# A planned two-layer graph kernel on one core: other landing costs and no chain between transfers in the plan, another form of one gated update, and one gate moved ahead

## The chip, the core and the metric

The kernel runs on one core of a Trainium2 chip. The metric is device microseconds of one launch, as the median of a few runs; lower is better. A core has five engines that work side by side, each through its own list of instructions in order: PE (TensorE, matrix products), DVE (VectorE), ACT (ScalarE), POOL (GpSimd) and SP (SyncE, which here only issues transfers). Transfers (DMAs) are issued by SP, ACT or POOL and then run by themselves; an engine that needs the data waits for a semaphore. Because each list is worked in order, an instruction that waits also holds up everything behind it on the same engine.

## What is computed

Thirty-two sequences `x[b]` of 512 nodes with 128 features go through two layers that share one 512 x 512 adjacency matrix. Layer 0 is a graph attention layer, layer 1 a gated graph network of five steps. Each has a layer norm and a ReLU in front and a residual sum behind. Cut to what matters:

```python
h = jnp.maximum(_layernorm(x, axis=-1), 0.0)
x = x + _L0_gnn_ref(h, adj, ...)              # softmax over neighbours, then a weighted mean
h = jnp.maximum(_layernorm(x, axis=-1), 0.0)
def step(h, _):                               # five times
    m_in = jnp.einsum('nm,bmd->bnd', in_matrix, h)
    m_out = jnp.einsum('nm,bmd->bnd', out_matrix, h)
    av = jnp.concatenate([m_in, m_out], axis=-1)
    u3 = h @ u3_w.T + u3_b
    z = jax.nn.sigmoid(av @ w3_w.T + w3_b + u3)
    r = jax.nn.sigmoid(av @ w4_w.T + w4_b + u3)
    hv = jnp.tanh(av @ w5_w.T + w5_b + (r * h @ u5_w.T + u5_b))
    h = (1.0 - z) * h + z * hv
    return (h, None)
x = x + h
```

Both matrices of the second layer are the same adjacency matrix, so the kernel forms one product `m` and adds the weight halves beforehand.

## The kernel before

**One step of one sequence.** A step is called by `recurrence(b, step, ...)` (L1012); below, (8, 1) means sequence 8, step 1. The state is kept twice: as `hT` (features in the partitions, f32, scaled by `LIFT`), and as rows split into two f16 parts, `hi` and `lo`, whose sum stands for the f32 value. In order, a step does this:

- PE: `m` from four products with `hi` and four with `lo` (L1031). ACT copies it to `mT` (L1042).
- PE: the r gate, `g` from `u3T` with `hT` and `w4sT` with `mT` (L1050, L1051). ACT takes its tanh, `rs` (L1056). DVE makes `rh` (L1063).
- PE: the z gate, by adding `w3dT` with `mT` onto the same bank once `rs` has been read (L1071). ACT takes its tanh, `zs` (L1078).
- PE: the candidate `v` from `w5sT` with `mT` and `u5hT` with `rh` (L1089, L1090). ACT takes its tanh, `hv` (L1095).
- DVE: three full-width instructions, `d = LIFT*hv - hT` (L1101), `d = (zs+1)*d` (L1107), `hT = 0.5*d + hT` (L1110). The gates are tanh forms, so that (tanh+1)/2 is the sigmoid.
- The new `hT` must be turned back into rows for the next step's `hi` and `lo` (L1008, L1006).

The turning is done in two ways. In the first steps and in the last two steps of the last four sequences, PE transposes `hT` into a PSUM bank (L1124). Everywhere else (146 times) it goes by way of DRAM: DVE transposes blocks of 32 (L1137, `blocks`), SP stores them to a DRAM buffer (L1143, `way`), and SP loads them back in four parts (L1148, `rows`). After the last step the result is scaled by `1/LIFT`, added to the kept input `x1s` and stored (L1172 to L1188).

**Layer 0** of a sequence (`layer0`, L763) feeds the recurrence. From the fifth sequence on its transposes also go through DRAM, issued by POOL: `blockwise` (L717) stores four parts (L733) and loads them back (L746), and the attention scores are spread with four small stores (L866) and one load (L879).

**The last sequence** ends in `ending` (L1191) in halves. Its result is summed in a PSUM bank: `kept`, the part `(zs-1)*hT` (L1201), is turned by products with the matrix `minus` (L1211); `gated`, the part `(zs+1)*hv` (L1234), is turned by products with `plus` (L1241).

**What sets the order.** No order is written out by hand. `add` collects tasks, each with an engine, a cost from `COST`, a key, its needs and its buffers. `plan` (L83) then plays them through and puts out the order in which they begin. At each turn it looks, engine by engine, for tasks whose needs are met and whose buffers are free, and takes among those that can begin soonest the one with the lowest key. A task's result counts as seen at its planned end plus `lands`; for a transfer that is `LANDING`, 2600 ns (L48):

```python
seen = begin + t.ns + t.lands
...
heir.at = max(heir.at, begin + t.ns if heir.engine == t.engine == "PE" else seen)
```

The order so found is then pinned on every engine. It is only an order: on the chip each instruction waits for its true needs, not for the planned time. In the plan each of the four loads of `rows` needs the load before it to have landed:

```python
needs.append(add("SP", [1], keys(6), load(g), (t, *needs[-1:]), (way, f),
                 lands=LANDING))
```

and the four stores of `blockwise` (L742) and of the scores (L875) are chained in the same way. On the chip no such wait exists, since the parts don't touch each other; the chain only spreads them out in the order.

Of the kernel before, what the change touches and what calls it, by code (L numbers as in the profile page):

```python
# [13 lines left out]
ALU = mybir.AluOpType  # L14

P = 128
# [6 lines left out]
LIFT = 4096.0  # L23
# [4 lines left out]
SLOTS = 10  # L28
# [6 lines left out]
EARLY_NORMS = ("a1", "a2", "a3", "b0")  # L35
ADJ_LANDS = 5600
HALVED = 1
STEP = 6100
LEAD = 11
COST = {  # L40
# [4 lines left out]
    "SP": (430, 0, 0),  # L45
}
FIRST_IDLE, IDLE = 32, 36
LANDING = 2600  # L48
BRANCH = 150

WAIT = {"DVE": 200, "ACT": 200}
# [232 lines left out]
def gat_then_gated_gnn_kernel(  # L284
# [20 lines left out]
    nc = tc.nc  # L305
    B, N, D = x.shape
    K = N // P
# [14 lines left out]
    pin = tc.keep_in_program_order  # L322
    tasks = []

    def add(*args, **kwargs):
        tasks.append(Task(*args, **kwargs))
        return tasks[-1]

    def new(buffer, name, shape=(P, N)):
        tag = buffer.tags[0]  # L330
        if "bank" in buffer.tags:
            buffer.tile = psum.tile([P, N], F32, tag="bank", name=name)
        elif tag in ("way", "turn", "line"):
# [35 lines left out]
    x1s = [state.tile([P, K, D], F32, name=f"x1_{s}") for s in range(SLOTS)]  # L369
# [85 lines left out]
    t = add("PE", [1024], soon, issue, (a_dst_loaded,), (f_as,), at=4300)  # L455
# [56 lines left out]
    t = add("POOL", [1] * 3, 0, issue, (rest_loaded,))  # L512
# [9 lines left out]
    t = add("PE", [256] * 5, 0, issue, (t,), (f_ws, f_us))  # L522
# [55 lines left out]
    t = add("DVE", [1] * 4, late, issue, (*counted, wa_made))  # L578
# [138 lines left out]
    def blockwise(dst, src, which, keys, needs, buffers, by_halves):  # L717


        f, way = Buffer("blocks"), Buffer("turn")  # L720

        def blocks():
            pin(nc.vector.transpose(
                new(f, f"blocks_{which}"), src().rearrange("p k d -> p (k d)")
            ))

        t = add("DVE", [512], keys(0), blocks, needs, (*buffers, f))

        def store(g):
            def issue():  # L730
                if way.tile is None:
                    new(way, f"turn_{which}", (K * P, P))
                pin(nc.gpsimd.dma_start(  # L733
                    out=way.tile.rearrange("(e r) (g q) -> g r e q", r=Q, g=G)[g],
                    in_=f.tile[ts(g, Q)].rearrange("r (e q) -> r e q", q=Q),
                ))

            return issue

        stores = []  # L740
        for g in range(G):
            stores.append(add("POOL", [1], keys(1), store(g), (t, *stores[-1:]), (f, way),  # L742
                              lands=LANDING))

        def load():
            pin(nc.gpsimd.dma_start(  # L746
                out=dst().rearrange("p (k m) -> p k m", k=K),
                in_=way.tile.rearrange("(k p) m -> p k m", k=K),
            ))

        return add("POOL", [1], keys(2), load, stores, (*buffers, way), lands=LANDING + 1500)

    finished = {}

    def due(b):

# [6 lines left out]
    def layer0(b):  # L763
# [7 lines left out]
        def keys(i):  # L771
            return begin + length * (base[0] + i) / parts
# [61 lines left out]
        if direct:  # L834
            f_es = Buffer("g", "bank")

            def spread(half):
                def issue():
                    es = f_es.tile or new(f_es, f"es_{b}")
                    for k in range(2 * half, 2 * half + 2):  # L840
                        pin(nc.tensor.transpose(
                            es[:, ts(k, P)], hw()[:, k, D + 1 : D + 2].to_broadcast([P, P]), ident
                        ))

                return issue

            t = None
            for half in range(2):
                t = add("PE", [256] * 2, keys(0), spread(half), (made[half], t), (f_hw, f_es))
        else:  # L850
            f_es, f_lines, way = Buffer("es"), Buffer("lines"), Buffer("line")
            rep = Q // K

            def gather():
                pin(nc.vector.transpose(
                    new(f_lines, f"lines_{b}", (P, Q)).rearrange("p (k e) -> p k e", k=K),
                    hw()[:, :, D + 1 : D + 2].to_broadcast([P, K, rep]),
                ))

            t = add("DVE", [64], keys(0), gather, made, (f_hw, f_lines))  # L860

            def store(k):
                def issue():
                    if way.tile is None:
                        new(way, f"line_{b}", (K, P))
                    pin(nc.gpsimd.dma_start(  # L866
                        out=way.tile[k].rearrange("(g q) -> g q", g=G),
                        in_=f_lines.tile[k * rep :: Q],
                    ))

                return issue

            stores = []
            for k in range(K):
                stores.append(add("POOL", [1], keys(1), store(k), (t, *stores[-1:]),  # L875
                                  (f_lines, way), lands=LANDING))

            def spread():
                pin(nc.gpsimd.dma_start(  # L879
                    out=new(f_es, f"es_{b}"),  # L880
                    in_=way.tile.rearrange("k p -> (k p)").partition_broadcast(P),
                ))

            t = add("POOL", [1], keys(2), spread, stores, (way, f_es), lands=LANDING + 1500)
        base[0] = 15
# [126 lines left out]
    def recurrence(b, step, halved, turned):  # L1012
# [5 lines left out]
        def keys(i):  # L1018
            return key + i * STEP / 4

        hT = hTs[b % SLOTS]
# [51 lines left out]
            ))  # L1073

        t = add("PE", [2048], keys(3), gate_z, (t_r,), (f_g, f_mT))

        def tanh_z():
            pin(nc.scalar.activation(  # L1078
# [11 lines left out]
            pin(nc.tensor.matmul(v, lhsT=u5hT, rhs=f_rh.tile, start=False, stop=True))  # L1090

        t = add("PE", [2048] * 2, keys(3), candidate, (t_rh,), (f_v, f_mT, f_rh))

        def tanh_v():
            pin(nc.scalar.activation(new(f_hv, f"hv_{b}_{step}"), f_v.tile, AF.Tanh, bias=vb))  # L1095

        t = add("ACT", [512], keys(4), tanh_v, (t,), (f_v, f_hv))


        def differ():  # L1100
# [8 lines left out]
        def update():  # L1109
            pin(nc.vector.scalar_tensor_tensor(hT, f_d.tile, 0.5, hT, ALU.mult, ALU.add))  # L1110

        t = add("DVE", [512], keys(5), differ, (t,), (f_hv, f_d))
        t = add("DVE", [512], keys(5), gated, (t, t_z), (f_z, f_d))
        turned = add("DVE", [512], keys(5), update, (t,), (f_d,))

        nth = 5 * b + WIDTH * step
        if nth < 5 * SHORT or (step >= STEPS - 2 and b >= B - SHORT_END):

            f = Buffer("o", "bank")

            def turn():
                h_ps = new(f, f"h_{b}_{step}")
                for k in range(K):
                    pin(nc.tensor.transpose(h_ps[:, ts(k, P)], hT[:, ts(k, P)], ident))  # L1124

            needs = (add("PE", [256] * K, keys(6), turn, (turned,), (f,)),)
            view = ("p k d -> p k d", {})

            def src():
                return f.tile.rearrange("p (k d) -> p k d", k=K)  # L1130
        else:


            f_b, way, f = Buffer("blocks"), Buffer("way"), Buffer("rows")

            def blocks():
                pin(nc.vector.transpose(  # L1137
                    new(f_b, f"blocks_{b}_{step}").rearrange("p (g k q) -> p g k q", g=G, k=K),
                    hT.rearrange("p (k g q) -> p g k q", g=G, k=K),
                ))  # L1140

            def store():
                pin(nc.sync.dma_start(out=new(way, f"way_{b}_{step}"), in_=f_b.tile))  # L1143

            def load(g):
                def issue():
                    rows = f.tile or new(f, f"rows_{b}_{step}", (P, G, N // G))
                    pin(nc.sync.dma_start(  # L1148
                        out=rows[ts(g, Q)],
                        in_=way.tile.rearrange("(a q) (g e) -> g q a e", a=G, g=G)[g],  # L1150
                    ))

                return issue

            t = add("DVE", [512], keys(6), blocks, (turned,), (f_b,))
            t = add("SP", [1], keys(6), store, (t,), (f_b, way), lands=LANDING)
            needs = []
            for g in range(G):
                needs.append(add("SP", [1], keys(6), load(g), (t, *needs[-1:]), (way, f),
                                 lands=LANDING))  # L1160
            view = ("p k (a q) -> p a k q", {"a": G})

            def src():
                return f.tile.rearrange("p a (k q) -> p a k q", k=K)
# [11 lines left out]

        def result_at_once():
            pin(nc.vector.scalar_tensor_tensor(
                new(f_res, f"res_{b}", (P, K, D)), src(), 1 / LIFT, x1s[b % SLOTS], ALU.mult,
                ALU.add,  # L1180
            ))

        if view[1]:
# [148 lines left out]
```

## Time and profile before

| what | value |
|---|---|
| median of three runs | 1145.57 us (1143.91 to 1149.21) |
| the profiled execution, its own time | 1144.8 us |
| its span, first to last instruction | 1142.7 us |
| PE busy | 1133.5 us (99%), 4373 instructions |
| DVE busy | 940.6 us (82%), 2124 instructions |
| ACT busy | 659.9 us (58%), 1297 instructions |
| POOL busy | 350.0 us (31%), 503 instructions |
| granted TensorE clock, mean | 1.000 |
| SP's transfers, by packets' time | 26.5% of 16 DMA engines |
| POOL's transfers, by packets' time | 13.0% of 16 DMA engines |
| `way` stores, `rows` loads | 146 of 256 KB, 584 of 64 KB |

Busy time is counted from the records of one execution on the chip. A wait names what came last before the engine went on. Matmul records overlap, since they are pipelined; a long stretch of busy PE says that nothing kept it waiting, not that it ran at its peak.

### The profile page before, as it was taken

The numbers are of one execution on the slowest core, as the hardware profiler recorded it, in microseconds if no ns is written. First come the engines' busy times: TensorE is split into PE (matmuls) and PEld (weight loads), VectorE is DVE, ScalarE is ACT, GpSimd is POOL, SyncE is SP. The second block draws the span as 40 slices with busy tenths as digits, with TensorE's granted clock in tenths as the row PEclk, the third lists the DMA queues.
The fourth block names the chain that finished last, engine by engine and source line by source line (L and its number), as shares of the span: only waits on it lengthen the run. The fifth ranks groups of instructions, "written<-read, shape, count | busy, mean of one in ns | idle before, by whom it ended". The sixth has DMA issues, their size and how long they took to land.

```text
span 1142.7 us, 15158 instructions
## 1 busy us (share of the span) xinstructions
PE 1133.5 (99%) x4373; PEld 598.5 (52%) x4373; DVE 940.6 (82%) x2124; ACT 659.9 (58%) x1297; POOL 350.0 (31%) x503
## 2 busy tenths in 40 slices
PE   9999999999999999999999999999999999999998
PEld 8665554554555545555554555555555555444444
DVE  7888887887879979889898888799889988667664
ACT  6665656456556465647556646655655655555553
POOL 4345434123244143244413242432544331100000
PEclk9999999999999999999999999999999999999999
DMA  3114444344354444344543443452455343322311
GB/s 107 44 38 122 115 128 133 112 146 118 104 164 116 136 130 136 116 138 119 146 136 115 126 132 120 139 154 89 133 149 144 116 121 117 107 92 79 102 44 67
DMA packets 133916, 132.88 MB, mean 116 GB/s; under 512 B 22083, under 2 KB 97989, under 8 KB 133701
## 3 DMA queue, kind: packets, MB, share of 16 engines
q1 hardware_dynamic: 116066, 94.89, 26.5%
q0 software_dynamic: 17472, 36.79, 13.0%
q8 instruction: 36, 0.59, 0.2%
q14 instruction: 52, 0.42, 0.1%
q10 hardware_dynamic: 290, 0.20, 0.1%
HBM read 70.39 MB, written 61.40 MB: 115 GB/s over the span
## 4 chain that ended last, share of the span: by engine, by line
PE 91%; DVE 5%; DMA 2%; issue 1%; ACT 0%; SPq 0%; DVEq 0%; ACTq 0%
PE m L1031 23%; PE g L1071 11%; PE v L1090 11%; PE g L1050 11%; PE v L1089 11%; PE g L1051 11%; PE av L922 9%; PE hp L806 2%; DMA rows<-way 1%; DVE hT L1110 1%; DVE pt L891 1%; DVE blocks L1137 1%; DVE lo L1006 1%; PE h L1124 1%; DVE d L1101 0%
## 5 line engine op out<-in xcount | busy, mean ns | idle before, releaser
L1056 ACT ACTIVATE rs<-g,zrb 128x512 f32<-128x512 f32 x160 | 109.7, 686 | 143.9 <-PE g L1051 133.4
L1101 DVE SCALAR_TENSOR_TENSOR d<-hv,hT 128x512 f32<-128x512 f32 x159 | 108.4, 682 | 78.3 <-ACT hv L1095 78.0
L1095 ACT ACTIVATE hv<-v,vb 128x512 f32<-128x512 f32 x159 | 108.8, 684 | 104.8 <-PE v L1090 104.2
L1042 ACT COPY mT<-m 128x512 f32<-128x512 f32 x160 | 93.6, 585 | 123.7 <-PE m L1031 121.1
L1031 PE MATMUL m<-adjT,hi 128*128 128x512 f16 x640 | 162.6, 379 | 1.8 <-ACT hi L1008 1.8
L1050 PE MATMUL g<-hT,u3T 128*128 128x512 f32 x320 | 163.5, 593 | 0.0
L1051 PE MATMUL g<-mT,w4sT 128*128 128x512 f32 x320 | 163.5, 592 | 0.0
L1071 PE MATMUL g<-mT,w3dT 128*128 128x512 f32 x320 | 163.1, 593 | 0.0
L1031 PE MATMUL m<-adjT,lo 128*128 128x512 f16 x640 | 162.1, 379 | 0.4 <-DVE lo L1006 0.4
L1089 PE MATMUL v<-mT,w5sT 128*128 128x512 f32 x318 | 162.4, 592 | 0.0
L1090 PE MATMUL v<-rh,u5hT 128*128 128x512 f32 x318 | 162.4, 592 | 0.0
L1078 ACT ACTIVATE zs<-g,zrb 128x512 f32<-128x512 f32 x160 | 109.6, 686 | 59.6 <-PE g L1071 56.6
L1063 DVE SCALAR_TENSOR_TENSOR rh<-rs,hT 128x512 f32<-128x512 f32 x160 | 108.6, 682 | 40.8 <-ACT rs L1056 40.3
L922 PEld LDWEIGHTS av<-hw,pt 128*128 128x128 f32 x1024 | 122.0, 191 | 17.8 <-issue 13.6
L922 PE MATMUL av<-hw,pt 128*128 128x129 f32 x1024 | 123.2, 275 | 0.2 <-ACT adjT L497 0.2
L1110 DVE SCALAR_TENSOR_TENSOR hT<-d,hT 128x512 f32<-128x512 f32 x159 | 109.7, 690 | 11.3
L1031 PEld LDWEIGHTS <-hi 128*128 128x128 f16 x640 | 62.5, 98 | 103.0 <-issue 46.7
L1107 DVE SCALAR_TENSOR_TENSOR d<-zs,d 128x512 f32<-128x512 f32 x159 | 109.6, 689 | 4.5
L1137 DVE STREAM_TRANSPOSE blocks<-hT 128x512 f32<-128x512 f32 x146 | 102.7, 706 | 5.3 <-DMA way<-blocks 3.2
L1031 PEld LDWEIGHTS <-lo 128*128 128x128 f16 x640 | 62.4, 98 | 84.7 <-issue 14.2
L644 POOL TENSOR_TENSOR rs_b<-ve_b,mhalf 128x4 f32<-128x4 f32 x32 | 37.2, 1162 | 224.7 <-DVE ve_b L624 188.4
L1051 PEld LDWEIGHTS g<-mT,w4sT 128*128 128x128 f32 x320 | 60.7, 190 | 76.7 <-issue 71.5
(135 smaller groups left out, 1443.7 us busy)
## 6 DMA issues: line engine op xcount, KB each, us to landing
way<-blocks SPq DMA_DIRECT2D x146, 256.0 KB, 2.1
rows<-way SPq DMA_DIRECT2D x584, 64.0 KB, 2.1
x<-in_x_dram SPq DMA_DIRECT2D x32, 256.0 KB, 2.9
out_dram<-res SPq DMA_DIRECT2D x31, 256.0 KB, 2.1
turn_a<-blocks_a POOLq DMA_DIRECT2D x112, 64.0 KB, 2.3
h0T<-turn_a POOLq DMA_DIRECT2D x28, 256.0 KB, 3.5
es<-line POOLq DMA_DIRECT2D x28, 256.0 KB, 3.8
turn_b<-blocks_b POOLq DMA_DIRECT2D x112, 64.0 KB, 2.3
```

What stands on the lines that cost most here:

```text
L922: pin(nc.tensor.matmul(avs()[:, i, :], lhsT=f_pts[c].tile[:, ts(2 * part + i, P)], rhs=hw()[:, c, : D + 1], start=start, stop=(c == K - 1) ...
L1031: pin(nc.tensor.matmul(f_m.tile, lhsT=part[:, k, :], rhs=adjT[:, k, :], start=(first and k == 0), stop=(not first and k == K - 1),))
L1050: pin(nc.tensor.matmul(g, lhsT=u3T, rhs=hT, start=True, stop=False))
L1051: pin(nc.tensor.matmul(g, lhsT=w4sT, rhs=f_mT.tile, start=False, stop=True))
L1056: pin(nc.scalar.activation(new(f_r, f"rs_{b}_{step}"), f_g.tile, AF.Tanh, bias=rb, scale=0.5))
L1071: pin(nc.tensor.matmul(f_g.tile, lhsT=w3dT, rhs=f_mT.tile, start=False, stop=True, skip_group_check=True))
L1078: pin(nc.scalar.activation(new(f_z, f"zs_{b}_{step}"), f_g.tile, AF.Tanh, bias=zb, scale=0.5))
L1089: pin(nc.tensor.matmul(v, lhsT=w5sT, rhs=f_mT.tile, start=True, stop=False))
L1090: pin(nc.tensor.matmul(v, lhsT=u5hT, rhs=f_rh.tile, start=False, stop=True))
L1107: pin(nc.vector.scalar_tensor_tensor(d, f_z.tile, 1.0, d, ALU.add, ALU.mult))
L1110: pin(nc.vector.scalar_tensor_tensor(hT, f_d.tile, 0.5, hT, ALU.mult, ALU.add))
L1137: pin(nc.vector.transpose(new(f_b, f"blocks_{b}_{step}").rearrange("p (g k q) -> p g k q", g=G, k=K), hT.rearrange("p (k g q) -> p g k q", ...
```

## The change

Three things are changed.

- **The plan's transfers.** `LANDING` goes from 2600 to 5000 ns, for all transfers that use it. The chain is taken off the four loads of `rows`, off the four stores of `blockwise` and off the four score stores: each now needs only the data it moves. All orders of all engines come out of the plan anew.
- **The update of sequence 30 in its last step** (`near`; sequence 31 takes `ending`). Instead of `d`, `d`, `hT`, three instructions in a row of which the first needs `hv`, it makes `kept = (zs-1)*hT` as soon as `zs` is there, then `hv = (zs+1)*hv`, then `kept = LIFT*hv - kept`. That is twice the new state; it is turned from the `d` buffer, and the result is scaled by `0.5/LIFT`.
- **The last sequence's z gate** in the last step becomes a need of sequence 30's candidate, so that PE does it first.

```diff
+NEAR = 2
...
-LANDING = 2600
+LANDING = 5000
...
-            stores.append(add("POOL", [1], keys(1), store(g), (t, *stores[-1:]), (f, way),
+            stores.append(add("POOL", [1], keys(1), store(g), (t,), (f, way),
                               lands=LANDING))
...
-                stores.append(add("POOL", [1], keys(1), store(k), (t, *stores[-1:]),
+                stores.append(add("POOL", [1], keys(1), store(k), (t,),
                                   (f_lines, way), lands=LANDING))
...
         t = add("PE", [2048], keys(3), gate_z, (t_r,), (f_g, f_mT))
+        if last and b == B - 1:
+
+            candidates[b - 1].needs.append(t)
+            candidates[b - 1].missing += 1
+            t.heirs.append(candidates[b - 1])
...
         t = add("PE", [2048] * 2, keys(3), candidate, (t_rh,), (f_v, f_mT, f_rh))
+        candidates[b] = t
...
+        near = last and b >= B - NEAR
...
-        t = add("DVE", [512], keys(5), differ, (t,), (f_hv, f_d))
-        t = add("DVE", [512], keys(5), gated, (t, t_z), (f_z, f_d))
-        turned = add("DVE", [512], keys(5), update, (t,), (f_d,))
+
+
+        def keep():
+            pin(nc.vector.scalar_tensor_tensor(
+                new(f_d, f"kept_{b}"), f_z.tile, -1.0, hT, ALU.add, ALU.mult
+            ))
+
+        def gated_hv():
+            hv = f_hv.tile
+            pin(nc.vector.scalar_tensor_tensor(hv, f_z.tile, 1.0, hv, ALU.add, ALU.mult))
+
+        def twice():
+            pin(nc.vector.scalar_tensor_tensor(
+                f_d.tile, f_hv.tile, LIFT, f_d.tile, ALU.mult, ALU.subtract
+            ))
+
+        if near:
+            t_keep = add("DVE", [512], keys(3.5) - STEP, keep, (t_z,), (f_z, f_d))
+            t = add("DVE", [512], keys(5), gated_hv, (t, t_z), (f_z, f_hv))
+            turned = add("DVE", [512], keys(5), twice, (t, t_keep), (f_hv, f_d))
+            to_turn = f_d
+        else:
+            t = add("DVE", [512], keys(5), differ, (t,), (f_hv, f_d))
+            t = add("DVE", [512], keys(5), gated, (t, t_z), (f_z, f_d))
+            turned = add("DVE", [512], keys(5), update, (t,), (f_d,))
+            to_turn = None
...
-                needs.append(add("SP", [1], keys(6), load(g), (t, *needs[-1:]), (way, f),
+                needs.append(add("SP", [1], keys(6), load(g), (t,), (way, f),
                                  lands=LANDING))
...
-                new(f_res, f"res_{b}", (P, K, D)), src(), 1 / LIFT, x1s[b % SLOTS], ALU.mult,
-                ALU.add,
+                new(f_res, f"res_{b}", (P, K, D)), src(), (0.5 if near else 1) / LIFT,
+                x1s[b % SLOTS], ALU.mult, ALU.add,
```

More of the change, by code (lines that the diff above doesn't have):

```diff
@@ L751, in blockwise @@
         return add("POOL", [1], keys(2), load, stores, (*buffers, way), lands=LANDING + 1500)
-    finished = {}
+    finished, candidates = {}, {}
     def due(b):
@@ L1122, in turn @@
                 h_ps = new(f, f"h_{b}_{step}")
+                h = to_turn.tile if to_turn else hT
                 for k in range(K):
-                    pin(nc.tensor.transpose(h_ps[:, ts(k, P)], hT[:, ts(k, P)], ident))
-            needs = (add("PE", [256] * K, keys(6), turn, (turned,), (f,)),)
+                    pin(nc.tensor.transpose(h_ps[:, ts(k, P)], h[:, ts(k, P)], ident))
+            needs = (add("PE", [256] * K, keys(6), turn, (turned,),
+                         (f, to_turn) if to_turn else (f,)),)
             view = ("p k d -> p k d", {})
```

## The prediction

> **What bounds the kernel now.** I read the page first (shares, granted clock, chain), then PE's waits, then the timeline round the longest wait on three engines, then the end.
>
> ```profile
> PE 1133.5 (99%) x4373; PEld 598.5 (52%) x4373; DVE 940.6 (82%) x2124; ACT 659.9 (58%) x1297; POOL 350.0 (31%) x503
> ...
> PE 91%; DVE 5%; DMA 2%; issue 1%; ACT 0%; SPq 0%; DVEq 0%; ACTq 0%
> ```
>
> ```profile
> PE m L1031 <- ACT hi L1008: 1.8, 1, 1.8
> PE idle L434 <- POOL ident masks.py:199: 1.4, 1, 1.4
> PE m L1031 <- DVE lo L1006: 0.4, 1, 0.4
> PE h L1124 <- DVE hT L1110: 0.2, 1, 0.2
> PE av L922 <- ACT adjT L497: 0.2, 1, 0.2
> ```
>
> PE is the bound, at a clock of 1.000, and is idle for 4.0 us in five places (columns: total, times, longest). What remains of the 9.2 us between PE's busy time and the span is the 5.2 us after its last product: the last results on DVE, the last stores, the closing of the program. The change takes no product away. So whatever the plan does, it can win the waits of 1.8 and 0.4 us, a little at the end, and nothing else; the 1.4 us at the start wait for the identity matrix, before any planned transfer.
>
> The long wait, engine by engine:
>
> ```profile
> 318.94 1.02 PE L1051 MATMUL g<-mT,w4sT 128*128 128x512 f32 x2
> 321.79 1.04 PE L1031 MATMUL m<-adjT,hi 128*128 128x512 f16 x4 [1.82 <-ACT hi L1008]
> ```
>
> ```profile
> 318.24 0.63 ACT L819 ACTIVATE hw<-hp,hw 128x128 f32<-128x128 f32 x2
> 320.60 0.63 ACT L1172 ACTIVATE res<-rows 128x512 f32<-128x512 f32 x1 [1.73 <-DMA rows<-way]
> 321.13 0.60 ACT L1008 CAST hi<-rows 128x512 f16<-128x512 f32 x1
> ```
>
> ```profile
> 304.04 0.40 SPq L1143 DMA_DIRECT2D way<-blocks  x1
> 305.22 2.28 SPq L1148 DMA_DIRECT2D rows<-way  x5
> 310.56 0.34 SPq L1143 DMA_DIRECT2D way<-blocks  x1
> 310.94 2.81 SPq L1148 DMA_DIRECT2D rows<-way  x3
> 315.20 0.34 SPq L1143 DMA_DIRECT2D way<-blocks  x1
> 315.59 1.45 SPq L1148 DMA_DIRECT2D rows<-way  x3
> ```
>
> The n-th record of a line in the trace is the n-th such instruction in the built order, so each can be given its sequence and step. PE waits for `hi` of (8, 1). Its `way` store is issued at 304.04; its first `rows` load at about 306.3, its fourth only at 316.1, and that lands at about 320.6. In between SP's list has the stores of (7, 2) and (6, 3), at 310.56 and 315.20, and each held the list until its own `blocks` existed. The four loads are apart because the plan chained them. Over all 118 such turnings before a further step, the first and fourth load are issued 7.7 us apart in the median (4.5 to 9.8 from tenth to ninetieth percentile), and SP spends 324 us in all waiting for `blocks`.
>
> ```profile
> way<-blocks SPq DMA_DIRECT2D x146, 256.0 KB, 2.1
> rows<-way SPq DMA_DIRECT2D x584, 64.0 KB, 2.1
> ```
>
> The transfer itself takes 2.1 us in the median.
>
> **What the Trainium skill says.** The page "DMA: Bandwidth & Descriptors", section "Anatomy of one DMA — SWDGE (gpsimd) path", gives a fixed cost of about 2.0 us plus bytes over 436 GB/s; for 64 KB my estimate from it is 2.15 us, and the trace has 2.1 (up to 4.9), also for SP's path. The same section says that a wait is held on the issuing sequencer, not by the DMA engines: that is the hold-up seen on SP. Section "Issuing engines are not separate DMA queues" says that SP's and POOL's transfers share the 16 engines; 26.5% and 13.0% of their time are taken here, so there is room on the mean, not always in a burst. "Perfetto Trace Analysis", "Optimization Strategy": look for the gaps of the contended engine and what ends them. That is the list above, and here it is short.
>
> **The change, part by part.** The built order of the changed kernel (no times in it) has the same number of instructions on PE, DVE and ACT, and it departs from the old one only after the start-up of the first four sequences.
>
> *Loads unchained, landing 5000.* In the old plan a `rows` transfer cost 430+2600 for the store and 4 x (430+2600) for the loads, 15.2 us. In the new one it is 430+5000 + 4 x 430+5000, 12.2 us. So the plan brings a sequence's next `m` nearer to its last `v`. I weigh PE's own work between the two in the built order (0.215 us per f16 product of 512 columns, 0.86 per f32 product, 0.22 per `av` or `hp` product, as they follow each other in the timeline; this adds up to 1131 us against 1133.5 busy). The shortest distance was 19.5 us and is now 17.2; the median goes from 29.8 to 29.0.
>
> What is needed across it: `hv` 0.9 (0.2 to begin, 0.69), three updates and `blocks` at 0.69 to 0.70 each, 2.8; SP and `way` landing 2.2; four loads, now next to each other, 1.5; the last landing; `hi` 0.65. The nearest rows for loads close together landed late: 2.8, 3.8 and 4.0 us after the last issue where the four came within 1.3 to 2.7 us. With 3.5 the sum is 11.6 us. So 5.7 us are left in the tightest place. Where another sequence's `way` stands between store and loads on SP, the loads wait for its `blocks`; this happened in 110 of 118 places, with a worst of 12.5 us between the two `v`, and is left in 55, with at most 4.3. Counting that too, the smallest slack is 4.1 us; the same sum for the old order is negative in just two places, and the worst of them is (8, 1). I take the 1.82 us as gone. Bounds: 0 (another place waits as long) to 1.82.
>
> The 0.43 us for `lo` at 926 are of another kind: DVE had an attention product and an update in its list before it. A new order may have the like elsewhere. I count 0, bounds -0.43 and +0.5.
>
> *POOL's stores unchained.* POOL is 31% busy. From `hp` to `av` the shortest PE distance goes from 22.9 to 21.5 us; from `av` to the first `m` from 10.7 to 10.3; from `av` to the first gate from 26.8 to 27.7. No PE wait came from there before, and the POOL stores no longer stand apart. Nothing, at most +1.
>
> *Closer neighbours.* A z gate may begin when `rs` is read: 0.2 + 0.69 + 0.06 = 0.95 us behind the r gate. The new order has four places at or under about 1 us: 0.86 (26, 0), 0.89 (17, 3), 1.00 (13, 3), 0.86 (31, 4). The old order had 0.86 and 0.97, without a recorded wait. The shortfalls add up to 0.24, taken as 0.2. In three of them four ReLU pieces (1.63 us together) stand ahead of `rs` on ACT: upper bound 3 x 1.6, about +4.9.
>
> *The end.* Before, from 1129.33 on, PE's list is z30, v30, z31, the halves of v31, `end` with `minus`, `h` of 30, `end` with `plus`. DVE:
>
> ```profile
> 1134.30 0.68 DVE L1107 SCALAR_TENSOR_TENSOR d<-zs,d 128x512 f32<-128x512 f32 x1
> 1135.02 0.69 DVE L1110 SCALAR_TENSOR_TENSOR hT<-d,hT 128x512 f32<-128x512 f32 x1
> 1135.81 0.76 DVE L1234 SCALAR_TENSOR_TENSOR gated<-zs,hv_end 128x256 f32<-128x256 f32 x2
> ```
>
> `h` waits for `hT` (0.17) and `gated` is behind it. After: z31 begins at 1130.25 (0.06 late, `rs` of 31), v30 ends at 1132.83, `hv` of 30 is there at 1133.7, two DVE instructions bring it to 1135.2; `gated` runs to 1135.96. PE is not held: `minus` from 1134.55 to 1135.6, `h` to 1136.03, `plus` to 1137.08, against 1137.34 before. `res` of 30, then the two last `res` halves, end at about 1137.8 instead of 1138.25. That is 0.4 us, bounds 0 and 0.6. The number of DVE instructions is the same; one of them (`kept`) goes under v30.
>
> **Sum** against the profiled execution: -1.8 - 0.4 + 0.2 = -2.0, so 1142.8 from 1144.8. The median of the runs is 0.8 above that execution, so 1143.6.
>
> **Rivals.**
>
> *The gain is eaten by new short waits* (1145.6). For it: a plan drawn anew, ACT's ReLU pieces ahead of `rs`, DVE at 82%. Against it: the old order had as close places and only 2.3 us of such waits in 1100.
>
> *Bursts land late and the run is slower* (1152). Four loads and four POOL stores now come at once, and each waiter has less distance. Place: `hi` at the head of ACT, where PE's work since the `v` is now 12.6 us at the least (14.6 before), while the last load lands after about 11. If bursts land at 6 us or more instead of 3.5, some dozen places hold ACT by 1 us or more, and the recurrence loses its slack where it is 4 to 6 us. That many at 0.7 us each are 8 or 9, less the 2 won: +6.5. It decides from a landing of about 7.5 us on; the longest on SP so far is 5.0.
>
> *Much faster* (1139): only if the 5.2 us at the end shrink or products follow each other more closely. Nothing in the profile speaks for it.
>
> *It doesn't do what it says:* the four loads could stay apart if the plan put others between. In the built order they stand together in 131 of 146 turnings (2 before), and elsewhere have one instruction between them, so this one is out.
>
> **How the numbers follow.** Forecast 0.60, eaten 0.22, slower 0.13, much faster 0.05. Differences within 0.5% (5.7 us) can't be told from no change here, where three runs of one kernel lie 5.3 us apart. The forecast and the eaten case are inside it. Faster 0.05, same 0.82, slower 0.13. The range goes from 1140.8 (every wait won, and a low set of runs) to 1148.0 (+4.9 less the gain, and a little of the runs' spread).
>
> **What would show it.** Right: no wait of `m` for `hi` over 0.5 us; the four `rows` of a turning issued within 2 us nearly everywhere; SP's time behind `blocks` for loads gone; DVE's last `gated` right behind `twice`; PE idle under 2.5 us before its last product. Wrong: PE waits for `hi` or `rs` in many places, `rows` landing over 5 us in the median, or a PE busy time that isn't 1133 us.

## The result, and the profile after

| | before | after |
|---|---|---|
| median of the runs compared (20 each) | 1145.57 us | 1141.82 us |
| lowest to highest run | 1143.59 to 1151.06 us | 1141.06 to 1144.24 us |
| ratio, with its 95% interval | | 0.9966 [0.9957, 0.9975] |
| the profiled execution, its own time | 1144.8 us | 1141.51 us |
| its span | 1142.7 us | 1139.7 us |
| from the first `av` product to the end of the last product | 1125.73 us | 1123.24 us |

The kernel became faster by 3.75 us, 0.3%, and the interval lies wholly below 1. That is inside the 0.5% of the forecast, on its lower side: 1141.8 where 1143.6 was predicted. The page of the kernel after, its busy times and its chain of waits:

```profile
PE 1133.1 (99%) x4373; PEld 599.0 (53%) x4373; DVE 946.9 (83%) x2124; ACT 659.3 (58%) x1297; POOL 350.7 (31%) x503
...
PE 99%; ACT 0%; DVE 0%; issue 0%; POOL 0%; POOLq 0%; DVEq 0%
```

PE does the same work in the same time, and the chain now lies on it from end to end: the DMA and DVE shares that stood there before (2% and 5%) are gone. The waits of PE after (total, times, longest):

```profile
PE idle L435 <- POOL ident masks.py:199: 1.4, 1, 1.4
PE av L923 <- ACT adjT L498: 0.2, 1, 0.2
PE end L1274 <- DVE gated L1267: 0.2, 1, 0.2
```

Both waits of `m`, for `hi` (1.8) and for `lo` (0.4), are gone. SP's list after, round the place whose list the prediction shows:

```profile
312.83 1.82 SPq L1181 DMA_DIRECT2D rows<-way  x4
315.66 0.34 SPq L1176 DMA_DIRECT2D way<-blocks  x1
320.21 1.73 SPq L1181 DMA_DIRECT2D rows<-way  x4
```

The four loads of a turning stand together. Over the 118 turnings, the first and the fourth load are issued 1.4 us apart in the median (7.7 before), and the last lands 7.1 us after the end of its `blocks` (12.6). The transfers themselves take what they took, by the page's table of DMA issues (median us from issue to landing at the end of the line):

```profile
way<-blocks SPq DMA_DIRECT2D x146, 256.0 KB, 2.0
rows<-way SPq DMA_DIRECT2D x584, 64.0 KB, 2.2
```

So loads next to each other land no later than those that stood apart: at the ninetieth percentile 3.1 us behind their issue, where it was 3.2. SP's whole wait for `blocks` did not fall (381 us, 324 before); what changed is how many loads stand behind another sequence's store: 55 of 118 turnings in the new order, by the prediction's count, and 110 in the old.

So the predicted picture is there in the main. Two things don't fit: the gain is larger than the sum, and the end is not shorter. The rest of this text asks why.

A word on measure. Records of PE overlap, so a short wait is partly hidden in them. Beside the recorded idle time, the excess of start-to-start distances over their usual value is used here: each product begins a fixed time (the median for the kind of product ahead of it) behind the one before it when nothing holds it. From 25 us on it adds up to 3.8 us before (2.65 of it at `m`, where the records show 2.25) and 1.4 us after.

### The profile page after: what moved, and what is told of

Same layout as the page of the kernel before. It is cut to its first block, busy times and chain, and to the rows that moved or that the text cites. A ratio compares the mean times of both kernels' runs of the same rounds, so it can differ in the third digit from the quotient of the medians.

```text
span 1139.7 us, 15186 instructions
## 1 busy us (share of the span) xinstructions
PE 1133.1 (99%) x4373; PEld 599.0 (53%) x4373; DVE 946.9 (83%) x2124; ACT 659.3 (58%) x1297; POOL 350.7 (31%) x503
## 4 chain that ended last, share of the span: by engine, by line
PE 99%; ACT 0%; DVE 0%; issue 0%; POOL 0%; POOLq 0%; DVEq 0%
PE m L1032 24%; PE g L1072 12%; PE g L1051 12%; PE g L1052 12%; PE v L1096 12%; PE v L1095 12%; PE av L923 10%; PE hp L807 3%; PE idle L435 1%; PE h L1156 0%; PE t_a L702 0%; PE t_b L702 0%; PE v_end L1256 0%; PE es L842 0%; PE end L1274 0%; PE at_ps L489 0%
## 5 line engine op out<-in xcount | busy, mean ns | idle before, releaser
L734 POOL DMA_DIRECT2D turn_b<-blocks_b x112 | 73.8, 664 | 91.0 <-DVE blocks_b L724 89.3
```

## The experiments

Each kernel was timed beside the kernel before. The ratio, given with its interval, is not the quotient of the two medians; for e1 that would be 0.9967.

| kernel | median us | before, beside it | ratio [95%] |
|---|---|---|---|
| e1, plan alone | 1141.67 | 1145.40 | 0.9974 [0.9967, 0.9981] |
| e2, end alone | 1145.74 | 1145.40 | 0.9997 [0.9987, 1.0007] |
| e3, chains off alone | 1150.40 | 1145.40 | 1.0042 [1.0026, 1.0057] |
| e4, landing 5000 alone | 1408.37 | 1145.40 | 1.2293 [1.2267, 1.2320] |
| e5, before, loads issued together | 1147.02 | 1146.05 | 1.0013 [1.0004, 1.0022] |
| e6, after, landing 3800 | 1145.53 | 1146.05 | 1.0000 [0.9992, 1.0008] |
| e8, after, warm-up planned shorter | 1144.65 | 1146.05 | 0.9991 [0.9984, 0.9999] |
| e9, as e8, end's halves in own tiles | 1145.05 | 1146.05 | 0.9995 [0.9986, 1.0005] |
| e10, e5 with four block buffers | 1144.19 | 1146.19 | 0.9988 [0.9980, 0.9996] |
| e11, e6 with four block buffers | 1141.50 | 1146.19 | 0.9962 [0.9949, 0.9975] |
| e12, after with four block buffers, less warm-up | 1140.91 | 1146.19 | 0.9957 [0.9944, 0.9970] |
| e13, before with four block buffers | 1144.20 | 1146.19 | 0.9988 [0.9982, 0.9995] |

The last section shows that a launch can start some 2.1 us later or earlier, whatever the plan. A median of few runs carries the chance of it, so the time between the first `av` and the last product of the profiled executions is given beside it below.

### Which part of the change

Plan alone: the new end is switched off in the kernel after.

```diff
-        if last and b == B - 1:
+        if False and last and b == B - 1:
...
-        near = last and b >= B - NEAR
+        near = False
```

> The three chains off and the landing at 5000, but the end as in the kernel before; the order is that of the changed kernel up to the last gates. Theory A (the time of the kernel before is made of late transfers that differ from run to run, and its profiled execution had few of them): nearly the whole gain, 3.0 to 3.6 us below the kernel before in the median, no wait of PE for hi or lo over 0.3 us in the profile, and runs closer together than those of the kernel before. Theory B (the plan wins only the 2.3 us of waits that the profile showed, the rest of the 3.7 us comes from the end): 2.0 to 2.5 us below.

End alone: the old plan under the new end.

```diff
-LANDING = 5000
+LANDING = 2600
...
-            stores.append(add("POOL", [1], keys(1), store(g), (t,), (f, way),
+            stores.append(add("POOL", [1], keys(1), store(g), (t, *stores[-1:]), (f, way),
...
-                needs.append(add("SP", [1], keys(6), load(g), (t,), (way, f),
+                needs.append(add("SP", [1], keys(6), load(g), (t, *needs[-1:]), (way, f),
```

(and the same for the score stores)

> The end of the changed kernel on the old plan; the order is that of the kernel before up to the last gates. Theory A: 0.3 to 0.6 us below the kernel before, the waits for hi and lo in the middle still there (1 to 4 us in all), runs as far apart as those of the kernel before. Theory B: 1.2 to 1.7 us below.

The plan alone gives 1141.67, what the whole change gives. The end alone gives a ratio of 0.9997 whose interval holds 1. In the traces, too, the new end is no shorter: from the z gate of sequence 30 to the last result it takes 8.92 us before, 8.94 after and 8.98 with the plan alone. So the gain is the plan's.

Then the plan's own two parts, each with the old end. Chains off, landing left at 2600:

```diff
-LANDING = 5000
+LANDING = 2600
...
-        near = last and b >= B - NEAR
+        near = False
```

> Chains off, landing left at 2600, old end. The plan now asks for less than the transfers need: PE's work between a v and the next m falls to 12.0 us in the tightest place, where 11.6 us are needed with a landing of 3.5. If the margin of the 5000 does the work: some waits for hi of 0.5 to 2 us each stay, and the time is between the kernel before and the plan alone, 0 to 2 us below the kernel before. If taking the stores of others from between the loads does it all: as the plan alone, 3.0 to 3.6 below.

Landing 5000, chains kept:

```diff
-                needs.append(add("SP", [1], keys(6), load(g), (t,), (way, f),
+                needs.append(add("SP", [1], keys(6), load(g), (t, *needs[-1:]), (way, f),
...
-        near = last and b >= B - NEAR
+        near = False
```

(the chains of POOL's stores are put back too)

> Landing at 5000 with the chains left, old end. The plan reckons 27 us for a turning by way of DRAM, more than it can hide, and leaves r and z gates without anything between them. If the landing alone were what helps: 2 to 3.5 us below the kernel before. If the chain has to go with it: slower than the kernel before by 5 to 25 us, PE waiting for rs and for hi.

Both expectations were missed. Chains off alone is 5.0 us slower than before. Waits of PE in that run:

```profile
PE g L1072 <- ACT rs L1057: 1.9, 4, 0.8
PE g L1051 <- DMA hT<-turn_b: 1.6, 3, 0.7
```

Landing alone is 263 us slower. PE is idle for 14% of the time, and its mean granted clock is 0.954: the same products keep it busy for 1212.5 us instead of 1133.5. Waits of PE in that run:

```profile
PE m L1032 <- ACT hi L1009: 112.7, 44, 8.4
PE g L1072 <- ACT rs L1057: 33.0, 45, 1.0
PE m L1032 <- DVE lo L1007: 24.5, 21, 3.8
```

With the chain, each of five links counts 5.4 us, 27.2 us for a turning that has about 29 us of products in the median to lie under; with the links apart the same number counts 12.2. With the chains off and 2600, as in e3, it counts 7.4 us: about the 7.1 us that are really needed in the median, and nothing over for a late one. So with two block buffers each part alone does harm. What exactly the plan of the landing alone does to its queues is open.

### Is it SP's hold-up?

The prediction gave the gain one cause: loads of one turning that stand behind other sequences' stores on SP. That can be taken out of the kernel before without a new plan. SP issues all four loads where it issued the first; the order on PE, DVE, ACT and POOL stays what it was.

```diff
-                    rows = f.tile or new(f, f"rows_{b}_{step}", (P, G, N // G))
-                    pin(nc.sync.dma_start(
-                        out=rows[ts(g, Q)],
...
+                    if g:
+                        return
+                    rows = new(f, f"rows_{b}_{step}", (P, G, N // G))
+                    for i in range(G):
+                        pin(nc.sync.dma_start(
+                            out=rows[ts(i, Q)],
...
```

> The kernel before, with one thing changed: where SP issued the first load of a turning it now issues all four. PE, DVE, ACT and POOL keep the old order, instruction for instruction; the old landing of 2600, the old chains and the old end stay in the plan. Theory A (what is lost before is lost on SP, where a load waits behind another sequence's store): the waits of PE for hi go, 2.5 to 3.5 us below the kernel before in the median, runs nearer to each other. Theory C (it takes the larger margin and the new order of PE and ACT): less than 1 us below.

The wait of 1.8 us for `hi` of (8, 1) is gone, and the kernel is not faster: 1.0013 [1.0004, 1.0022]. PE waits elsewhere:

```profile
PE av L922 <- DVE pt L891: 2.4, 4, 1.2
...
PE m L1031 <- DVE lo L1006: 0.6, 1, 0.6
```

Its longest wait, by the timeline of that run (the bracket holds the idle time before the row, and what ended it):

```profile
524.96 0.71 DVE L1137 STREAM_TRANSPOSE blocks<-hT 128x512 f32<-128x512 f32 x1 [1.67 <-DMA way<-blocks]
...
527.68 0.74 DVE L891 SCALAR_TENSOR_TENSOR pt<-es,hw,adjT 128x512 f32<-128x512 f32 x1
...
528.48 1.72 PE L922 MATMUL av<-hw,pt 128*128 128x129 f32 x13 [1.25 <-DVE pt L891]
```

PE is said to wait for `pt`, an attention product of DVE. But DVE had stood for 1.67 us just before, with `blocks` at the head of its list, until an earlier `way` store had landed: only then was one of the two block buffers free. All that is behind it in DVE's list is late by as much.

The same in a plan that differs from the one after in a single number:

```diff
-LANDING = 5000
+LANDING = 3800
```

> The changed kernel with the landing at 3800 in place of 5000. The shortest PE work between a v and the next m is 14.2 us (17.2 at 5000, 12.0 at 2600), and the smallest slack behind another sequence's store 0.6 us (4.1 at 5000), at a landing of 3.5. Theory A (a plan is as good as its margin over the late landings of a run): 0.5 to 2.5 us above the changed kernel in the median, with more spread; between it and the 1150.4 of the unchained plan at 2600. Rival (5000 is not special, any plan without the chain does as well, and 2600 was one bad draw of the order): within 0.5 us of the changed kernel.

Nothing is left of the gain: 1.0000 [0.9992, 1.0008]. DVE's waits for block buffers there:

```profile
DVE blocks L1170 <- DMA way<-blocks: 10.0, 8, 3.9
```

and the longest of them in the timeline:

```profile
229.12 0.69 ACT L1057 ACTIVATE rs<-g,zrb 128x512 f32<-128x512 f32 x1
...
230.59 0.71 DVE L1170 STREAM_TRANSPOSE blocks<-hT 128x512 f32<-128x512 f32 x1 [3.86 <-DMA way<-blocks]
231.22 0.65 DVE L1064 SCALAR_TENSOR_TENSOR rh<-rs,hT 128x512 f32<-128x512 f32 x1
...
231.92 1.12 PE L1096 MATMUL v<-rh,u5hT 128*128 128x512 f32 x2 [1.12 <-DVE rh L1064]
```

`rs` was there at 229.81, and `rh`, which needs it, starts 1.4 us later, behind a transpose that belongs to another sequence. PE's record names `rh`; the cause is a buffer for which DVE waited before that. Here the Trainium skill, "Perfetto Trace Analysis", section "Optimization Strategy", is to be read one engine further: it says that a repeated gap on the engine that should be saturated can mean too few buffers for the next tile. In this trace the gap is not on PE but on DVE, eight times for these 10.0 us, and doesn't repeat at one place.

Total of DVE's waits at block transposes until a store has landed, over all three lines (`blocks`, `blocks_a`, `blocks_b`): before 5.2 us, after 3.9, e1 5.1, e2 6.2, e3 15.3, e5 11.0, e6 11.7, e8 9.9, e9 9.9. The kernels without a gain have nearly all the larger sums, though before and e2 show that the sum alone doesn't rank them: it counts waits in which nobody was behind DVE, too.

### Are the block buffers the cause?

Four block buffers instead of two, while the plan still reckons with two: every engine's order remains what it was, and only the waits for the store's landing go. In the kernel of loads together:

```diff
+            n = 4 if tag == "blocks" else BUFFERS[tag]
-            buffer.tile = pools[BUFFERS[tag]].tile(list(shape), F32, tag=tag, name=name)
+            buffer.tile = pools[n].tile(list(shape), F32, tag=tag, name=name)
```

> The kernel with the loads together on the old plan, and four real block buffers where the plan still reckons with two; every engine's order is the same as without them. In the run with two, PE no longer waited for hi but for pt, and DVE had stood 11 us in all waiting for a block buffer whose store had not landed. Theory D (what costs time is DVE held at a block transpose until an earlier store has landed, with everything behind it late): DVE's waits for way at the block transposes go to about nothing, PE's waits for pt go, and the time falls by 2 to 4.5 us against the same kernel with two buffers, to 1142.5 to 1145. Rival C (the order of PE and ACT of the old plan is what costs): no more than 0.7 us.

and the same two lines in the kernel with landing 3800:

> The kernel with the landing at 3800, and four real block buffers on the same order. With two, DVE stood 11.7 us for block buffers and PE then waited 1.1 us for rh and 1.0 for pt. Theory D: those waits go and the time falls by 2 to 3.5 us, to that of the changed kernel within 1 us. Rival (the margin on the loads, 14.2 us between v and m, is what costs): no more than 0.7 us.

Both came down, to 1144.19 (2.8 below) and 1141.50 (4.0 below). Between the first `av` and the last product, which leaves the start out, the profiled executions gain 3.0 and 3.2 us: 1127.91 to 1124.87, and 1126.33 to 1123.13. With landing 3800 nothing is left of PE's waits but the start:

```profile
PE idle L436 <- POOL ident masks.py:199: 1.4, 1, 1.4
PE av L924 <- ACT adjT L499: 0.2, 1, 0.2
```

That kernel equals the one after. So a landing of 3800 is as good as 5000 as soon as the buffers are there, and what 5000 does beyond that is to put the block transposes where two buffers are enough. In the kernel after, the waits at them are few and hold nobody up. DVE's waits after:

```profile
DVE blocks_a L724 <- DMA way<-blocks: 2.1, 2, 1.5
...
DVE blocks L1170 <- DMA way<-blocks: 1.4, 1, 1.4
...
DVE blocks_b L724 <- DMA way<-blocks: 0.4, 1, 0.4
```

The same edit in the kernel before:

> The kernel before in its own order, with four real block buffers. Theory D alone: DVE's 5.2 us of waits for block buffers go, and most of the gain of the change with them, 2 to 3.5 us below the kernel before. If the hold-up on SP at (8, 1) is a cause beside it: that wait of PE for hi stays (1 to 2 us), and the time is 0 to 1.5 us below the kernel before; both must go for the whole gain.

1144.20 against 1146.19 beside it; by the ratio of 0.9988 some 1.4 us, by the quartiles of the runs 1.0 to 1.2 (1143.6 and 1145.6 against 1144.6 and 1146.8). Of this, 0.3 lies outside the span from the first to the last instruction. DVE's waits in the profiled execution of before:

```profile
DVE blocks L1137 <- DMA way<-blocks: 3.2, 3, 1.9
...
DVE blocks_a L723 <- DMA way<-blocks: 1.2, 2, 0.7
...
DVE blocks_b L723 <- DMA way<-blocks: 0.8, 1, 0.8
```

With four buffers these are gone, and what PE still waits for is:

```profile
PE m L1032 <- ACT hi L1009: 0.9, 1, 0.9
PE m L1032 <- DVE lo L1007: 0.6, 1, 0.6
PE g L1072 <- ACT rs L1057: 0.4, 1, 0.4
```

The wait for `hi` at 321 us is still there, at half its length, so the hold-up on SP makes it without the buffers' help. Between the first `av` and the last product the four buffers change nothing in this one execution (1125.73 and 1125.82). For the kernel before, then, what they win is shown by the times of the runs alone.

Nor are the two causes all. Kernel e10 has both taken away on the old order, and it does not reach the kernel after: 1144.19 against 1141.82, and 1124.87 against 1123.24 us between the first `av` and the last product. It is no lower than e13 by the medians (1144.20), though 1.0 us lower between those products. PE still waits there, beside the start:

```profile
PE m L1032 <- DVE lo L1007: 0.6, 1, 0.6
PE av L923 <- DVE pt L892: 0.4, 1, 0.4
```

The wait for `lo` is the one that the prediction saw at 926 us and counted as nothing. In the trace of before, DVE works without a pause up to it; `lo` only stands late in its list, behind an attention product:

```profile
924.67 0.75 DVE L891 SCALAR_TENSOR_TENSOR pt<-es,hw,adjT 128x512 f32<-128x512 f32 x1
925.33 0.68 DVE L1006 TENSOR_TENSOR lo<-hN,hi 128x512 f16<-128x512 f32 x1
926.07 1.04 PE L1031 MATMUL m<-adjT,lo 128*128 128x512 f16 x4 [0.43 <-DVE lo L1006]
```

No buffer and no issue on SP mends that; the new order does. By start-to-start distances PE's excess is 2.9 us in e10, between 3.8 before and 1.4 after. So 1.6 us (between first `av` and last product) to 2.4 us (by the medians) of the gain came with the new order beyond the two causes. Which of its moves bring them is not separated.

### The end, and a shorter warm-up

Two tries to better the kernel after. First, fewer of the transposes that keep PE warm (`idle`): the plan is told 25 instead of 36.

```diff
-FIRST_IDLE, IDLE = 32, 36
+FIRST_IDLE, IDLE = 32, 25
```

> The changed kernel with 25 in place of 36 warm-up transposes in the second group. The last eleven stand at 101 us and later in the changed kernel, where PE has work, and take 0.11 us each. If PE is the bound there, 1.0 to 1.3 us below the changed kernel. If they only fill time in which PE would wait, no difference (within 0.4 us).

Then, on top of it, own tiles for the two halves of the end, since they seemed to hold each other up:

```diff
-        f, f_p, f_res = Buffer("o", "bank"), Buffer("d"), Buffer("res")
+        f, f_res = Buffer("o", "bank"), Buffer("res")
+        f_vs, f_hvs = (f_v, Buffer("v", "bank")), (f_hv, Buffer("hv"))
+        f_ps = (Buffer("d"), Buffer("blocks"))
...
```

> As the one with 25, and the two halves of the last sequence get a bank, an hv and a gated tile each. In the profile of the changed kernel the first half of hv starts only when the last product of the second half is done, the first gated only after the second hv: the halves of the end wait for each other. If the shared tiles are why: the first hv starts about 1 us sooner, and the last result 0.3 to 0.5 us sooner, counted from the last z gate. If not: as the one with 25.

Eleven transposes fewer made it 2.8 us slower than after: the plan was drawn anew, and with it came waits of 0.8 for `pt`, 0.8 for `lo` and 0.4 for `rh`, with 9.9 us of DVE's waits for block buffers. A new plan moves several waits of this size; an edit of a planned kernel must be read against that.

Why the end brought nothing is seen in the kernel after itself. Its timeline:

```profile
1131.58 0.59 PE L1256 MATMUL v_end<-rh,u5hT 128*128 128x256 f32 x2
...
1132.27 0.84 ACT L1263 ACTIVATE hv_end<-v_end,vb 128x256 f32<-128x256 f32 x2 [1.04 <-PE v_end L1256]
1133.17 0.76 DVE L1267 SCALAR_TENSOR_TENSOR gated<-zs,hv_end 128x256 f32<-128x256 f32 x2 [0.49 <-ACT hv_end L1263]
...
1133.65 1.16 PE L1274 MATMUL end<-plus,gated 128*128 128x128 f32 x8 [0.15 <-DVE gated L1267]
```

The products of the first half of `v_end` end at 1131.30, yet its `hv_end` begins at 1132.27, after those of the second half (1132.17). The first `gated` likewise begins only after the second `hv_end` (1133.11). The product with `plus` then follows the first `gated`, which ends at 1133.60. With own tiles:

```profile
1134.17 0.47 ACT L1265 ACTIVATE hv_end<-v_end,vb 128x256 f32<-128x256 f32 x1 [0.18 <-PE v_end L1258]
...
1135.54 0.47 ACT L1265 ACTIVATE hv_end<-v_end,vb 128x256 f32<-128x256 f32 x1 [0.89 <-DVE kept L1132]
1135.93 0.76 DVE L1271 SCALAR_TENSOR_TENSOR gated<-zs,hv_end 128x256 f32<-128x256 f32 x2 [0.49 <-PE end L1246]
1136.42 1.16 PE L1278 MATMUL end<-plus,gated 128*128 128x128 f32 x8 [0.15 <-DVE gated L1271]
```

The first `hv_end` now follows its own product, which ends at 1134.07, by 0.1 us instead of 1.0; so the shared tile was what held it. But the second one is held until `kept` is done and both `gated` until the product with `minus` is, and PE waits the same 0.15 us. From the z gate of sequence 30 to the last result it is 8.94 us with and without own tiles. There are only two `hv` buffers, and `kept` is the last to read what one of them held before; that would explain the wait of the second `hv_end`. Neither wait was tested.

Last, without a new plan: the order of the kernel after, four block buffers, and the last eleven warm-up transposes, which stand at 101 us and later, not issued.

```diff
+            n = 4 if tag == "blocks" else BUFFERS[tag]
...
+        idles.append(0)
+        if len(idles) > 57:
+            return
```

> The changed kernel in its own order, with four real block buffers and without issuing the last eleven warm-up transposes, which stood at 101 us and later. Unlike the one with 25 in the plan, nothing else moves. If PE is the bound there, 1.0 to 1.3 us below the changed kernel (1141.8): 1140.5 to 1140.8. If they filled a wait, the same as the changed kernel within 0.4 us. The buffers by themselves bring little, since DVE waits only 3.9 us for them in the changed kernel and PE for nothing behind them.

1140.91, ratio 0.9957 [0.9944, 0.9970]. It is the lowest of all, and clearly below the kernel before. Against the kernel after it is 0.9 us lower by the medians, 1.0 between first `av` and last product (1122.2 against 1123.2), but the two intervals overlap.

## Why the prediction was right, and where its terms were not

The forecast case came: a small gain, from waits that go. Between the first `av` and the last product of the profiled executions it is 2.5 us, where the sum says 2.0; part of the larger difference of the medians is chance, as the offset below shows. Term by term:

- **Loads unchained, -1.82.** Right in kind, too small. The wait for `hi` is gone, and that for `lo`, which was counted as nothing won, went as well. By start-to-start distances 2.65 us at `m` became 0: the term was 0.8 short, 0.66 of it at `lo`. Its landing of 3.5 us for loads next to each other was too long: they took 2.2 in the median, and the longest 5.1. The page "DMA: Bandwidth & Descriptors", from which 2.15 was estimated, was nearer than the three late rows that were preferred to it.
- **The cause behind it** was read too narrowly. The prediction explained the one long wait rightly, by SP's list, and took it for nearly all there was. The runs show a second cause: DVE stands for block buffers. Taking SP's hold-up away alone won nothing (e5); giving four buffers alone won 1.0 to 1.4 us by the times (e13); both together on the old order stay 1.6 to 2.4 us short of the kernel after (e10), where `lo` and `pt` still stand late in DVE's list. The step that was too short is "What is needed across it", which counted `blocks` at 0.70 and no wait for its buffer. That the chosen plan needs few such waits (3.9 us of DVE, none that PE sees) was not foreseen: with a landing of 3800 the same sum leaves 0.6 us of slack in the worst place and so promises the same gain, which did not come (e6). In that the forecast was lucky.
- **POOL, nothing.** Right: no PE wait after comes from its transfers.
- **Closer z gates, +0.2.** Their excess went from 0.26 to 0.75 us, so +0.5; far from the upper bound of 4.9.
- **The end, -0.4.** It was 0 (8.92 and 8.94 us, above), and the sign named for it, the last `gated` right behind `twice`, did not come: DVE waited 0.49 us for `hv_end`. The failing step is the sum that let the halves run past each other, with `gated` ready at 1135.96 and the last product ending at 1137.08. The trace of before had it too; ACT stood free for 1.04 us until the second half's product was done:

```profile
1134.69 0.84 ACT L1230 ACTIVATE hv_end<-v_end,vb 128x256 f32<-128x256 f32 x2 [1.04 <-PE v_end L1223]
```

- **The offset, +0.8.** "The median of the runs is 0.8 above that execution" was carried over to the new kernel. After, the median is 0.3 above its profiled execution. The runs of before lie in two groups: of 162 timed in all, 39 lie between 1144 and 1145 us, 50 between 1146 and 1147, and only 20 in the microsecond between. Parted at 1145.6, their medians are 1144.5 and 1146.75, nearly as far apart as an early and a late start (2.1 us, last section). The profiled execution of 1144.8 belongs to the early group, and 1145.57 is a value between the two, not an offset of the kernel. After, 14 of 20 runs are in the early group, of median 1141.7, and the others have 1143.8. So early against early and late against late the gain is 2.8 to 3.0 us, and the rest of the 3.75 is the luck of how many runs started early. Which start a run had is inferred from its time.

Profile against profile the gain is 3.3 us: 2.5 between the first `av` and the last product (2.4 by the excess), 0.15 at the start, 0.3 behind the last product, 0.3 outside the span. The last two are hardly the plan's: e13, with the old order, is as far below before behind the last product (4.7 against 5.2 us) and outside the span (1.8 against 2.1).

The upper end of the range, 1148.0, does not come out of its terms: 4.9 in place of the 0.2 gives 1148.3.

Of the rivals, *eaten by new short waits* is real for other plans: e6 and e8 are just that. The kernel after escaped it. *Bursts land late* did not come: `rows` took 2.2 us in the median and 5.1 at most. The slower kernel e3 shows other waits: z gates that wait for `rs`, and 15.3 us of DVE at block transposes; how its 5 us divide between the two wasn't separated, and four buffers were not tried on it.

## What to carry to other kernels

When PE's record names a product of DVE or ACT, look at what that engine had at the head of its list just before: a wait for a buffer that a store's landing frees delays everything behind it, whoever it belongs to. In a kernel that is planned, a transfer's reckoned time sets where buffers are used again as well as when data is expected; before a new number for it, try more real buffers with the order held fixed, which tells the two apart. And when two causes are found, take both away at once on the old order: what is then still missing, as in e10, has another cause. Before a difference of 1 to 3 us in medians is explained, see whether the runs lie in groups, and compare like with like.

## What the runs showed of the hardware

PE's first products come at two speeds. At the start the warm-up transposes follow each other at 0.21 us, and then at 0.11. In the kernel after, the second group is already quick:

```profile
1.37 3.96 PE L435 MATMUL idle<-ident 128*128 128x128 f32 x18 [1.37 <-POOL ident masks.py:199]
...
5.88 1.31 PE L435 MATMUL idle<-ident 128*128 128x128 f32 x10
...
11.57 1.13 PE L923 MATMUL av<-hw,pt 128*128 128x129 f32 x8 [0.16 <-ACT adjT L498]
```

In e2 the same ten take 2.40 us, and the first `av` comes 2.1 us later, though the instructions up to it are the same:

```profile
6.54 2.40 PE L435 MATMUL idle<-ident 128*128 128x128 f32 x10
...
13.70 1.13 PE L923 MATMUL av<-hw,pt 128*128 128x129 f32 x8 [0.16 <-ACT adjT L498]
```

The Trainium skill, "TensorE: Matmul & The Clock Gate", section "What's actually happening", describes a clock that is halved until PE has been busy for one window of about 3.4 us; the window runs freely, so that the change comes at another time in each run. The halved spacing agrees. The page of a profile doesn't show it (its mean clock is 0.999 after and 1.000 in e2), but the clock records in the traces do: the full clock begins at 5.0 us in the kernel after and at 9.8 in e2. Over the fourteen profiled executions it begins between 4.1 and 6.1 us in ten and between 9.8 and 10.8 in four (e2, e4, e6, e10). The 2.1 us are what it costs here end to end: the 20 runs of the kernel after lie in two groups, 14 from 1141.1 to 1142.2 and 6 from 1143.7 to 1144.2, and e6 and e10 were profiled with the late start too (first `av` at 13.87 and 13.77). The profiled executions of e2 and e6, at 1145.77 and 1146.82, lie in the upper groups of their kernels. That these groups are the two starts is inferred from this and from the equal distance; only single executions have traces.

Grouping the runs has its limit, too. By groups e2, whose order is that of before up to the end, would be 0.9 to 1.3 us below before, with 4 and 10 runs, though its ratio holds 1. A difference of about 1 us between two kernels, such as the gain of e13, is therefore not sure to be the edit's unless a trace shows the wait that went.
